# Gate and up read their token operands in runs of 512 columns, their weight blocks and first loads are begun inside the attention's output product, and less of that product lies beside attention

## The chip, the cores and the metric

The kernel runs on one core of one Trainium2 chip. The metric is the device time of one execution in microseconds (us), and lower is better. The kernel is written in a tile framework: the program names tiles in pools (SBUF, or PSUM for the eight accumulator banks), and the framework puts each instruction on its engine's queue and inserts the waits. In the profile PE is the matrix engine, PEld its weight loads, DVE the vector engine, ACT the scalar engine, POOL the GpSimd engine, SP the engine that issues most DMA. The names with a q (SPq) are the DMA queue's own sequencer.

## What is computed

The reference is one adaptive-layernorm transformer block over 2 batches of 1024 tokens, 1024 features, 32 heads of 32:

```python
mod = silu(c) @ wmod                       # 6 vectors of 1024 for each batch: shift, scale, gate, twice
h   = layernorm(x) * (1 + scale1) + shift1
q, k, v = split(clip(h @ Wqkv.T, -8, 8))   # q and k are layernormed over all 1024 features
p   = softmax(q @ k.T / sqrt(32) + alibi_bias, causal)
x1  = x + gate1 * ((p @ v) @ Wout.T)
h2  = layernorm(x1) * (1 + scale2) + shift2
act = silu(h2 @ Wg.T * ag) * (h2 @ Wu.T * au)      # 2752 inner features; Wg, Wu, Wd hold only -1, 0 and 1
out = x1 + gate2 * (act @ Wd.T * ad)
```

## The kernel before

The work runs in five stages: the modulation and the qkv product of batch 0; attention, with the other products of the two batches woven between its matmuls; the rest of the attention's output product; gate and up of batch 0 and then of batch 1; and the down product.

**Seven products.** The qkv, output, gate and up products each cut a 2 x 2 block product into seven products of half-size operands (Strassen's form). The list `SEVEN` gives their order. A token operand (`TOKEN_OPS`, seven for 256 tokens: four blocks or differences of blocks of the transposed h2, and so on) is formed once, by `token_operands`, split into a rounded high part and a remainder (`hl`, a tile of 128 partitions x 2 parts x 4 k-blocks x 128 columns, two buffers) and stored to `hop2_dram` in HBM. Gate and up read it back as seven tiles `hs_0` to `hs_6` of 2 MB for each batch. Each holds one operand of all four pairs of token tiles (NJ = 4 pairs j of 256 tokens). In the kernel before, the order inside a partition of `hs` is part, j, k-block, column, so that a matmul's moving operand (one part, one k, all j) is four runs of 128 columns with gaps between them.

**Attention and the woven work.** The generator `dense_work` yields the output product (`output`) for the four pairs of batch 0 and then the first two pairs of batch 1. `together` pulls from it according to `share`: DENSE0 and DENSE1 are how many us of such work, by the kernel's own count, are put beside each batch's attention. The rest of pairs (1,0) and (1,1) is finished when attention is over. Then `output` does pairs (1,2) and (1,3) alone. `operand(b, j)` loads the inverse softmax sums of a pair (`rb`, line 1202) and its attention outputs (`aoA`), multiplies them on DVE and POOL (line 1220), and forms the seven blocks. The sums of the last attention block reach `rb` through a store, a load, the reciprocal, a store (`rec`) and a load.

**From output to gate-up.** After `seven`, `output` normalises the pair (line 723 is the last step) and queues four transposes (`todo`), behind which come the operands of the pair and their stores (`hl`, lines 1180 to 1182).

**Gate and up.** `gate_up(b)` loops over 11 pairs p of 256 inner features (the last has 192, so 96 columns a half). `stage(p)` loads 2 MB of gate and up weights into two `wst` tiles (three buffers). `weight_operands` forms their seven operands: A11, A12 and A22 are copies on ACT (line 1559), S1 to S4 are sums on POOL (line 1561). In batch 0 `ternary` looks on DVE whether the weights are -1, 0 or 1. In batch 1 it does the same for the down weights, `wdst`, loaded for it alone. Seven steps e then issue 8 matmuls for gate and 8 for up into the banks gx, gy, ux, uy: 112 matmuls a pair and 2464 over both batches. Results are combined on DVE and ACT (`gP`, line 1603) and stored to `act_dram`. `ident_r` (line 1522) is a rounded identity for two `exact` probes of hs_0, done after step 0 of the first pair.

**Down.** The 11 down weight blocks are loaded (`wds`, line 1663 and later for the rest, two buffers) and rounded to `wd` on POOL and DVE in turn. For each of 16 token tiles the activations `a` are loaded on ACT's queue, split into `hi` (ACT, line 1678) and `lo` (DVE, line 1679), and 88 matmuls follow, whose moving operand is 512 contiguous columns of `wd`.

**Order.** Each engine works through its queue in order. While `pinned[0]` is true the matmuls keep program order; the framework sets the places of the other instructions. SP's loads and stores are one queue in order: one that must wait for a buffer holds up all behind it. A new tile in a used place waits for the last users of what lay there, with `reuse_waits="tile"` for the tile in question alone.

Of the kernel before, what the change touches and what calls it, by code (L numbers as in the profile page):

```python
# [480 lines left out]
def kernel(  # L481
# [81 lines left out]

    hop2_dram = [dram.tile([P, 7, 2, NJ, KC // 2, P], FP, tag=f"hs_{b}", name=f"hs_{b}") for b in range(B)]
    act_dram = [dram.tile([P, NJ, 2, NIC, P], FP, tag=f"act_{b}", name=f"act_{b}") for b in range(B)]
# [219 lines left out]
    def weights_b(pool, w, nm, sums, other=None, swap=False):  # L785
# [8 lines left out]
            )  # L794
            for q in order
        }
# [371 lines left out]
    def token_operands(b, j, h2, pool):  # L1168


        b11, b12, b21, b22 = (h2[:, ds(kh * KC // 2, KC // 2), m, :] for kh in range(2) for m in range(2))
        t = {q: pool.tile([P, KC // 2, P], FP, tag=f"t{q}", name=f"t{q}_{b}_{j}") for q in ("T1", "T2", "T3", "T4")}
        nc.vector.tensor_sub(t["T1"], b12, b11)
        nc.vector.tensor_sub(t["T2"], b22, t["T1"])
        nc.gpsimd.tensor_sub(t["T3"], b22, b12)
        nc.gpsimd.tensor_sub(t["T4"], b21, t["T2"])
        t.update(B11=b11, B21=b21, B22=b22)
        for i, q in enumerate(TOKEN_OPS):
            hl = pool.tile([P, 2, KC // 2, P], FR, tag="hl", name=f"hl_{b}_{j}_{q}", bufs=2)
            nc.vector.tensor_copy(hl[:, 0], t[q])  # L1180
            (nc.gpsimd if i % 2 else nc.vector).tensor_sub(hl[:, 1], t[q], hl[:, 0].bitcast(FP))
            nc.sync.dma_start(hop2_dram[b][:, i, :, j], hl.bitcast(FP))

# [52 lines left out]

    def output(b, js, pools, banks, bt, todo, keep, q0=1):

# [8 lines left out]
        for j in js:  # L1247
# [37 lines left out]
            yield from seven(lambda q, i: a[q][:, i, :], bt, banks, read, todo.places(q0, 1, ahead), 2)  # L1285
            yield from todo.run(len(todo.list), True)
            for m in range(2):
                nc.sync.dma_start(x1_dram[b * NT + qts[m]], xs[m])
# [14 lines left out]
    OUT_US = 112.0  # L1303
    LEAD, DENSE0, DENSE1 = 16.0, 345.0, 161.0

# [123 lines left out]
    ]  # L1429
    pinned[0] = True  # L1430
    ost = ctx.enter_context(ExitStack())
    right = {}
# [6 lines left out]
    def dense_work():  # L1439
        yield from dense0  # L1440
        yield from projections(1, qpools, banks, 1)
        early.close()
        hbp = right["hb"] = ost.enter_context(tc.tile_pool(name="hb", bufs=1))
        wop = ost.enter_context(tc.tile_pool(name="wo", bufs=1))
        gap_, tkp, partp, osm, aop = [
            ost.enter_context(tc.tile_pool(name=n, bufs=k))
            for n, k in (("oga", 1), ("tok", 4), ("opart", 1), ("osmall", 1), ("ao", 1))
        ]
        opools = (gap_, aop, tkp, partp, hbp, osm)
        operands(0, 0, opools[1])  # L1450
        bt = weights_b(wop, wout_t, "o", wt_dram[3])
        out_args.extend((opools, banks, bt, Todo(banks), keep))
        yield from output(0, range(NJ), *out_args)
        yield from output(1, range(NJ // 2), *out_args)
# [14 lines left out]
    opools, _, bt, todo, _ = out_args  # L1469
    with tc.tile_pool(name="wide", bufs=1, side="right") as wide:  # L1470
        operands(1, NJ // 2, opools[1], wide)
        in_range()
        alone(output(1, range(NJ // 2, NJ), *out_args, 3))
        alone(todo.run(len(todo.list), True))
    ost.close()
    late_pools.close()
# [32 lines left out]

    with ExitStack() as ff:  # L1510
        turns = [0]
        ffp = ff.enter_context(tc.tile_pool(name="ff", bufs=1, space=PSUM))
        BANKS = 8

        def ffbank(nm):
            turns[0] += 1
            i = (turns[0] - 1) % BANKS
            return ffp.tile([P, 512], FP, tag=f"ff{i}", name=nm)

        fcp = ff.enter_context(tc.tile_pool(name="fconst", bufs=1))  # L1520
        ident_r = fcp.tile([P, P], FR, name="ident_r")
        nc.vector.tensor_copy(ident_r, ident)

        with ExitStack() as gu:
            hsp = gu.enter_context(tc.tile_pool(name="hs", bufs=1, side="right", reuse_waits="tile"))
            wsp, stp, ptp, grp, urp, jkp = (
                gu.enter_context(tc.tile_pool(name=n, bufs=k, reuse_waits="tile"))
                for n, k in (("wops", 10), ("wst", 3), ("fpart", 1), ("gres", 2), ("ures", 3), ("junk", 1))
            )
            W_ORDER = ("A11", "A12", "S2", "S1", "S3", "S4", "A22")  # L1530

            def tokens_in(b, i, eng=nc.sync):
                t = hsp.tile([P, 2, NJ, KC // 2, P], FR, tag=f"hs{i}", name=f"hs_{b}_{i}")
                eng.dma_start(t.bitcast(FP), hop2_dram[b][:, i])
                return t

            def stage(p, eng=nc.sync):
                r0, n = PAIRS[p]
                st = []
                for kh in range(2):  # L1540
                    t = stp.tile([P, 2, KC // 2, 2 * P], FP, tag="wst", name=f"wst_{p}_{kh}")
                    for i, w_t in enumerate((wg_t, wu_t)):
                        eng.dma_start(
                            t[:, i, :, 0 : 2 * n],
                            w_t[ds(kh * D // 2, D // 2), ds(r0, 2 * n)].rearrange("(k p) f -> p k f", p=P),
                        )
                    st.append(t)
                return st

            def weight_operands(p, st, b):  # L1550
# [4 lines left out]
                }  # L1555
                W = {q: wsp.tile([P, 2, KC // 2, P], FR, tag="w", name=f"w{q}_{b}_{p}") for q in W_ORDER}
                f = {q: v.rearrange("p a k f -> p (a k) f")[:, :, 0:n] for q, v in W.items()}
# [14 lines left out]
            def gate_up(b):  # L1572
                tiles = [None] * 7
                st = [stage(0)]
                for i in range(7):
                    tiles[i] = tokens_in(b, i)
                for p in range(NPR):
                    n = PAIRS[p][1]
                    if p + 1 < NPR:
                        st.append(stage(p + 1))  # L1580
# [6 lines left out]
                    bank = {(mat, c_): ffbank(f"{mat}{c_}_{b}_{p}") for mat in "gu" for c_ in "xy"}  # L1587
                    part = {}
                    for e, (c_, qa, qb_, q) in enumerate(SEVEN):
                        done = {}  # L1590
                        for i, mat in enumerate("gu"):
                            ps = bank[mat, c_]
                            for k in range(KC // 2):
                                for hl in range(2):
                                    matmul(
                                        ps[0:n].rearrange("p (j t) -> p j t", j=NJ), W[qa][:, i, k, 0:n],
                                        tiles[e][:, hl, :, k, :],
                                        start=(q in ("P1", "P2", "P5") and k == 0 and hl == 0),
# [13 lines left out]
                        if q in QUAD:  # L1612
# [16 lines left out]
                            )  # L1629
                        if b == 0 and p == 0 and e == 0:  # L1630
                            exact(tiles[0][:, 0, 0].rearrange("p k t -> p (k t)"), NCOUNT, ffbank("probe0"), jkp)
                            exact(tiles[0][:, 1, 0].rearrange("p k t -> p (k t)"), NCOUNT + 1, ffbank("probe1"), jkp)
                            turns[0] += 2

            for b in range(B):
                gate_up(b)

        with ExitStack() as dn:
            wdp, wdst, aip, hip, lop, xp1, yp, dlp = (
                dn.enter_context(tc.tile_pool(name=n, bufs=k, reuse_waits="tile"))  # L1640
                for n, k in (
                    ("wd", 1), ("wdst", 2), ("ain", 2), ("ahi", 2), ("alo", 2), ("x1in", 2), ("yout", 2), ("dlate", 1),
                )
            )
            gb = []
            for b in range(B):
                gb.append(dlp.tile([P, D], FP, name=f"gb{b}"))
                nc.scalar.dma_start(gb[b], gate_dram[5][b].partition_broadcast(P))
            wd = []
            for p, (r0, n) in enumerate(PAIRS):  # L1650
                t = wdst.tile([P, 2, D], FP, tag="wdst", name=f"wds_{p}")
                nc.sync.dma_start(t[0:n], wd_t[ds(r0, 2 * n), :].rearrange("(m p) e -> p m e", p=n))
                w = wdp.tile([P, 2, D], FR, tag=f"wd{p}", name=f"wd_{p}")
                (nc.vector if p % 2 else nc.gpsimd).tensor_copy(w[0:n], t[0:n])
# [3 lines left out]
            def more_wd():  # L1658
                for p, (r0, n) in enumerate(PAIRS):
# [3 lines left out]
                    nc.sync.dma_start(t[0:n], wd_t[ds(r0, 2 * n), :].rearrange("(m p) e -> p m e", p=n))  # L1663
                    w = wdp.tile([P, 2, D], FR, tag=f"wd{p}", name=f"wd_{p}")
                    (nc.vector if p % 2 else nc.gpsimd).tensor_copy(w[0:n], t[0:n])
# [39 lines left out]


    work.close()
    wrong = nc.values_load(bad_i[0:1, 0:1], min_val=0, max_val=1)
# [48 lines left out]
```

## Time and profile before

| | |
|---|---|
| Time, median of 3 runs | 2469.14 us (2466.67 to 2471.86) |
| The profiled execution's own time | 2464.6 us |
| Its span in the trace | 2462.9 us (1.7 us lie outside it) |
| Mean granted clock of PE over the span | 0.956 |
| PE | 2230.4 us busy, 91% of the span, 9715 matmuls |
| DVE | 1316.0 us, 53% |
| POOL | 936.4 us, 38% |
| ACT | 812.5 us, 33% |
| DMA | 441.56 MB in 249820 packets, 179 GB/s mean |

The profile's page gives busy time, a picture of the span in 40 slices of 61.6 us (each digit the busy share in tenths), the chain of work that ended last, and groups of instructions. Around it the trace can be asked for a timeline (start, duration, engine, line, operation, output and inputs, count; in brackets the idle time ahead of it and what ended it) and for windows (for each stretch the busy time of every engine, the granted clock, the DMA share and GB/s). Consecutive matmuls of one kind are one row of a timeline. The matmuls' ends are modelled, so the time of one in a steady stream is read from the starts of rows. Landmarks of the profiled execution: attention's last matmul ends at 1350.7 us, the first gate matmul starts at 1491.2, the second batch's gate-up starts near 1790 to 1800, gate-up ends at 2091.4, the first down matmul starts at 2107.2.

### The profile page before, as it was taken

The numbers are of one execution on the slowest core, as the hardware profiler recorded it, in microseconds if no ns is written. First come the engines' busy times: TensorE is split into PE (matmuls) and PEld (weight loads), VectorE is DVE, ScalarE is ACT, GpSimd is POOL, SyncE is SP. The second block draws the span as 40 slices with busy tenths as digits, with TensorE's granted clock in tenths as the row PEclk, the third lists the DMA queues.
The fourth block names the chain that finished last, engine by engine and source line by source line (L and its number), as shares of the span: only waits on it lengthen the run. The fifth ranks groups of instructions, "written<-read, shape, count | busy, mean of one in ns | idle before, by whom it ended". The sixth has DMA issues, their size and how long they took to land.

```text
span 2462.9 us, 27003 instructions
## 1 busy us (share of the span) xinstructions
PE 2230.4 (91%) x9715; PEld 1220.5 (50%) x9715; DVE 1316.0 (53%) x1909; ACT 812.5 (33%) x1667; POOL 936.4 (38%) x709
## 2 busy tenths in 40 slices
PE   6999999999999987988897657999999999499998
PEld 2444443333333322322222225788777887388887
DVE  5775642555656432676776575777535644222221
ACT  1322224444444454545454002333323332011110
POOL 2330213332545544756665554433434431211111
PEclk9999999999999998999899877999999999799999
DMA  9886867355266217454541559434486452833331
GB/s 365 308 317 249 301 236 248 101 186 191 82 204 202 82 57 262 149 160 134 162 148 63 157 213 341 125 116 124 163 303 196 147 164 75 303 121 125 127 126 36
DMA packets 249820, 441.56 MB, mean 179 GB/s; under 512 B 12769, under 2 KB 170049, under 8 KB 238669
## 3 DMA queue, kind: packets, MB, share of 16 engines
q1 hardware_dynamic: 242840, 407.71, 48.4%
q10 hardware_dynamic: 6836, 32.03, 3.6%
q8 instruction: 79, 1.29, 0.2%
q14 instruction: 65, 0.52, 0.1%
HBM read 305.46 MB, written 134.23 MB: 179 GB/s over the span
## 4 chain that ended last, share of the span: by engine, by line
PE 38%; DMA 5%; DVE 5%; issue 5%; POOL 5%; ACT 1%; SPq 0%; POOLq 0%; DVEq 0%; ACTq 0%
PE dn L739 11%; PE gx L739 6%; PE ux L739 6%; PE uy L739 4%; PE gy L739 4%; PE bank L739 4%; DMA wds<-in_L_ffn_Wd_dram 2%; PE sc L739 1%; DMA wst<-in_L_ffn_Wu_dram 1%; DVE p L1097 1%; PE av L739 1%; DMA hs<-hl_T 1%; POOL xr L1283 1%; ACT p L1065 1%; DVE h2t L845 1%
## 5 line engine op out<-in xcount | busy, mean ns | idle before, releaser
L1065 ACT ACTIVATE p<-sc,kw 128x128 f32<-128x128 f32 (+3 forms) x1024 | 422.7, 514 | 425.3 <-PE sc L739 395.2
L739 PE MATMUL bank<-wT,a 128*128 128x512 f32 x768 | 365.4, 609 | 13.9 <-ACT P L957 8.2
L1097 POOL TENSOR_TENSOR p<-p,p 128x1024 f32<-128x1024 f32 (+3 forms) x128 | 267.5, 2090 | 214.1 <-PE av L739 187.8
L1097 DVE TENSOR_TENSOR p<-p,p 128x1024 f32<-128x1024 f32 (+3 forms) x192 | 240.5, 1266 | 127.8 <-POOL p L1069 68.3
L739 PE MATMUL bank<-wB,a 128*128 128x512 f32 x576 | 270.5, 606 | 1.5 <-DVE raw L964 0.7
L739 PE MATMUL dn<-wd,hi 128*128 128x512 f32 (+1 forms) x704 | 221.8, 397 | 28.3 <-ACT hi L1678 15.8
L739 PEld LDWEIGHTS bank<-wT,a 128*128 128x128 f32 x768 | 136.4, 191 | 198.3 <-issue 167.6
L739 PE MATMUL dn<-wd,lo 128*128 128x512 f32 (+1 forms) x704 | 220.0, 394 | 5.6 <-DVE lo L1679 5.6
L739 PE MATMUL sc<-cq,ck 32*128 32x512 f32 (+3 forms) x1536 | 189.0, 553 | 39.5 <-ACT p L1065 31.1
L1069 POOL TENSOR_SCALAR_AFFINE_SELECT p<-p 128x256 f32<-128x256 f32 x256 | 129.7, 518 | 193.8 <-ACT p L1065 183.3
L739 PE MATMUL av<-p,cv 128*32 128x512 f32 (+3 forms) x1536 | 173.8, 513 | 19.1 <-POOL p L1069 19.1
L739 PEld LDWEIGHTS bank<-wB,a 128*128 128x128 f32 x576 | 102.0, 189 | 145.8 <-issue 123.8
L1561 POOL TENSOR_TENSOR wS<-wst,wst 128x1024 fp32r<-128x1024 f32 (+1 forms) x22 | 51.9, 2359 | 311.1 <-DMA wst<-in_L_ffn_Wu_dram 198.3
L739 PEld LDWEIGHTS dn<-wd,hi 128*128 128x128 f32 (+1 forms) x704 | 133.7, 191 | 59.5 <-issue 16.2
L739 PEld LDWEIGHTS dn<-wd,lo 128*128 128x128 f32 (+1 forms) x704 | 134.1, 191 | 35.0 <-DVE lo L1679 6.3
L739 PEld LDWEIGHTS sc<-cq,ck 32*128 32x128 f32 x1536 | 64.1, 189 | 170.1 <-issue 100.5
L1696 POOL TENSOR_TENSOR y<-y,x 128x512 f32<-128x512 f32 x32 | 40.6, 1290 | 268.1 <-DVE y L1695 268.1
L1695 DVE TENSOR_TENSOR y<-dn,gb 128x512 f32<-128x512 f32 x32 | 20.6, 686 | 219.6 <-issue 196.7
L1678 ACT CAST hi<-a 128x2560 fp32r<-128x2560 f32 (+1 forms) x32 | 42.3, 1369 | 284.1 <-PE dn L739 225.3
L739 PE MATMUL gx<-hs,wA 128*128 128x512 f32 (+1 forms) x352 | 91.5, 403 | 24.0 <-ACT wA L1559 23.0
L739 PEld LDWEIGHTS av<-p,cv 128*32 128x32 f32 x1536 | 32.9, 109 | 150.1 <-issue 78.4
L739 PE MATMUL gx<-hs,wS 128*128 128x512 f32 (+1 forms) x352 | 91.4, 402 | 6.1 <-ACT gP L1603 4.8
(233 smaller groups left out, 3382.4 us busy)
## 6 DMA issues: line engine op xcount, KB each, us to landing
a<-hop SPq DMA_DIRECT2D x20, 1792.0 KB
hs<-hs SPq DMA_DIRECT2D x14, 2048.0 KB
wm<-in_L_wmod_dram SPq DMA_DIRECT2D x48, 512.0 KB
wB<-in_L_attn_Wqkv_dram SPq DMA_DIRECT2D x21, 1024.0 KB
wst<-in_L_ffn_Wg_dram SPq DMA_DIRECT2D x40, 512.0 KB
wst<-in_L_ffn_Wu_dram SPq DMA_DIRECT2D x40, 512.0 KB
a<-act ACTq DMA_DIRECT2D x16, 1280.0 KB
qk<-qs SPq DMA_DIRECT2D x16, 1024.0 KB
```

What stands on the lines that cost most here:

```text
L739: return in_order(nc.tensor.matmul(*args, **kw_))
L845: nc.vector.tensor_scalar(dst(k), tp[:, j, :], mul(k), add(k), ALU.mult, ALU.add)
L1065: last_exp[0] = nc.scalar.activation(p[:, g, lo:hi], sp[:, g, lo:hi], AF.Exp, bias=kw[:, d, h_ : h_ + 1])
L1069: last_mask[0] = nc.gpsimd.affine_select(out=p[:, :, 0:P], in_=p[:, :, 0:P], pattern=[[0, 2], [1, P]], compare_op=ALU.is_ge, fill=0.0, bas ...
L1097: adders[b](half, jb).tensor_add(dst, dst, ps[half][:, :, 0:n])
L1283: nc.gpsimd.tensor_add(xs[m][:, ts(n, HALF)], xs[m][:, ts(n, HALF)], yg)
L1561: nc.gpsimd.tensor_add(f["S1"], raw["A21"], raw["A22"])
L1678: nc.scalar.copy(hi[v[0], v[1]], a[v[0], v[1]])
L1695: nc.vector.tensor_mul(y[:, ts(n, HALF)], pss[n], gb[b][:, ts(n, HALF)])
L1696: nc.gpsimd.tensor_add(y[:, ts(n, HALF)], y[:, ts(n, HALF)], x1[:, ts(n, HALF)])
```

## The change

It has nine parts.

1. `hop2_dram` and `hs` are laid out part, k-block, j, column. A matmul of gate-up now takes `tiles[e][:, hl, k, :]`, 512 contiguous columns. The store of one `hl` puts down runs of 128 columns (512 bytes), where before each partition's part was one run of 2 KB.
2. DENSE1 goes from 161 to 133.
3. The pools of the output stage are ordered anew: `osmall`, `hb` and `tok` in `low`, the rest in `ost`. The weight blocks of `weights_b` are allocated in reverse. The pool `wide` and the separate `operands(1, NJ // 2)` ahead of the last outputs go, so that pair (1,2) is taken ahead inside pair (1,1), as the others are.
4. `stage(0)` is issued, and the pools of weights and partial results opened, ahead of the last outputs.
5. The loads of hs_0 to hs_5 are issued by `first_tokens`, called inside the last `output` after its `seven`, ahead of that pair's stores of x1 and its layernorm; hs_6 is allocated after the outputs.
6. `wst` has two buffers in place of three, and each of the seven weight operands one buffer of its own in place of ten in rotation.
7. In batch 0, matmuls are not pinned until pair 1; the two probes move from pair 0 to pair 1.
8. PSUM for gate-up is two pools of four banks, the first open during the outputs.
9. The pools of the down stage lie on the right, in the place of gate-up's, and in another order.

The core of the diff:

```diff
-    hop2_dram = [dram.tile([P, 7, 2, NJ, KC // 2, P], FP, ...) for b in range(B)]
+    hop2_dram = [dram.tile([P, 7, 2, KC // 2, NJ, P], FP, ...) for b in range(B)]
...
-            for q in order
+            for q in (reversed(order) if made else order)
...
-            nc.sync.dma_start(hop2_dram[b][:, i, :, j], hl.bitcast(FP))
+            nc.sync.dma_start(hop2_dram[b][:, i, :, :, j], hl.bitcast(FP))
...
             yield from todo.run(len(todo.list), True)
+            if after is not None and j == NJ - 1:
+                after()
...
-    LEAD, DENSE0, DENSE1 = 16.0, 345.0, 161.0
+    LEAD, DENSE0, DENSE1 = 16.0, 345.0, 133.0
...
-    with tc.tile_pool(name="wide", bufs=1, side="right") as wide:
-        operands(1, NJ // 2, opools[1], wide)
-        in_range()
-        alone(output(1, range(NJ // 2, NJ), *out_args, 3))
-        alone(todo.run(len(todo.list), True))
-    ost.close()
+    in_range()
+    ff = ctx.enter_context(ExitStack())
+    gu = ctx.enter_context(ExitStack())
+    ffp = [ff.enter_context(tc.tile_pool(name="ff_a", bufs=1, space=PSUM))]
+    stp, wsp, ptp, grp, urp = (
+        gu.enter_context(tc.tile_pool(name=n, bufs=k, side="right", reuse_waits="tile"))
+        for n, k in (("wst", 2), ("wops", 1), ("fpart", 1), ("gres", 2), ("ures", 3))
+    )
...
+    staged = [stage(0)]
...
+    def first_tokens():
+        ost.close()
+        hsp = gu.enter_context(tc.tile_pool(name="hs", bufs=1, side="right", reuse_waits="tile"))
+        token_tiles(range(6), hsp)
+
+    alone(output(1, range(NJ // 2, NJ), *out_args, 3, first_tokens))
+    alone(todo.run(len(todo.list), True))
...
-                W = {q: wsp.tile([P, 2, KC // 2, P], FR, tag="w", name=f"w{q}_{b}_{p}") for q in W_ORDER}
+                W = {q: wsp.tile([P, 2, KC // 2, P], FR, tag=f"w{q}", name=f"w{q}_{b}_{p}") for q in W_ORDER}
...
+                    if p == 1:
+                        pinned[0] = True
...
+                    if (b, p) == (0, 1):
+                        for i, mat in enumerate("gu"):
+                            exact(tiles[0][:, i, 0], NCOUNT + i, bank[mat, "y"], jkp)
...
-                                        ps[0:n].rearrange("p (j t) -> p j t", j=NJ), W[qa][:, i, k, 0:n],
-                                        tiles[e][:, hl, :, k, :],
+                                        ps[0:n], W[qa][:, i, k, 0:n], tiles[e][:, hl, k, :],
...
-            wdp, wdst, aip, hip, lop, xp1, yp, dlp = (
-                dn.enter_context(tc.tile_pool(name=n, bufs=k, reuse_waits="tile"))
+            wdst, wda, yp, xp1, gbp, _, hip, lop, wdb = (
+                dn.enter_context(tc.tile_pool(name=n, bufs=k, side="right", reuse_waits="tile"))
                 for n, k in (
-                    ("wd", 1), ("wdst", 2), ("ain", 2), ("ahi", 2), ("alo", 2), ("x1in", 2), ("yout", 2), ("dlate", 1),
+                    ("wdst", 2), ("wda", 1), ("yout", 2), ("x1in", 2), ("gb", 1), ("gap", 1),
+                    ("ahi", 2), ("alo", 2), ("wdb", 1),
                 )
             )
```

## The prediction

> **What bounds the kernel now.** I read the slices first, then the windows between attention and gate-up, then the timeline of PE at every idle stretch. The slices (PE, granted clock):
>
> ```profile
> PE   6999999999999987988897657999999999499998
> PEclk9999999999999998999899877999999999799999
> ```
>
> PE is the bound nearly everywhere (2230.4 of 2462.9 us), so matmul time counts in full, and so do the holes: slices 22 to 24 (output to gate-up) and 34 (gate-up to down). The timeline of PE names what ended each hole (start, length, instruction, in brackets the idle time before it):
>
> ```profile
> 1386.36 9.12 PE L739 MATMUL bank<-wB_o,aoA 128*128 128x512 f32 x16 [21.92 <-DVE aoA L1220]
> 1457.53 1.09 PE L742 MATMUL bank<-ident,xr 128*128 128x128 f32 x4 [9.20 <-DVE xr L723]
> 1491.18 3.78 PE L739 MATMUL gx<-hs,wA 128*128 128x512 f32 x8 [22.56 <-ACT wA L1559]
> 1500.72 1.22 PE L739 MATMUL probe<-hs,ident_r 128*128 128x512 f32 x2 [3.26 <-DVE ident_r L1522]
> 2107.21 1.19 PE L739 MATMUL dn<-wd,hi 128*128 128x512 f32 x2 [15.82 <-ACT hi L1678]
> ```
>
> Then the steady streams. Between starts of rows in gate-up, and in down:
>
> ```profile
> 1600.26 2.04 PE L739 MATMUL uy<-hs,wS 128*128 128x512 f32 x8
> 1602.14 2.03 PE L739 MATMUL gx<-hs,wA 128*128 128x512 f32 x8
> 1604.01 2.04 PE L739 MATMUL ux<-hs,wA 128*128 128x512 f32 x8
> ```
>
> ```profile
> 2200.13 0.62 PE L739 MATMUL dn<-wd,lo 128*128 128x512 f32 x2
> 2200.59 0.61 PE L739 MATMUL dn<-wd,hi 128*128 128x512 f32 x2
> 2201.04 0.62 PE L739 MATMUL dn<-wd,lo 128*128 128x512 f32 x2
> ```
>
> Gate-up: 1.874 us for 8, 234.3 ns each. Down: 0.453 for 2, 226.6 ns. Same shape, same granted clock 1.00; down's moving operand is contiguous, gate-up's is four runs.
>
> [...]
>
> **The change part by part**, against the profiled execution's 2464.6 us (4.5 below the median).
>
> *(a) Contiguous operands.* 2464 matmuls × (234.3 − 226.6) = **−19**. Bounds: 0 if the 7.7 ns come of something else (other stationary source, banks), −19 if all of it. The pair of 96 columns, with a quarter less weight to load but the same runs, still takes 230.7 to 233.4, so weight loads aren't the cause. Batch 1's first pair follows DMA, so I take −17.
>
> *(b) Fewer outputs beside attention.* Before, PE has 12.2 us of leftover output after attention (to 1364.4), then idles 21.92: the operand of (1,2) lands 35.6 us after attention ends (sums, store, reciprocal at 1360.21, store, load of `rb`). `rb` is an SP step that was late by itself:
>
> ```profile
> 1374.74 16.08 SPq L1202 DMA_DIRECT2D rb<-rec  x8
> ```
>
> After, the scheduled order leaves 14 matmuls of (1,0) and all 28 of (1,1) behind attention's last: 42 × 0.87 = 36.5 us plus transposes, about 39, so the 35.6 us are covered and the idle 21.92 goes. What remains open is how much attention shortens by giving up 28 matmuls = 24.5 us of PE. From 900 to 1352 PE is 85% busy, with waits on ACT p 29.6 and POOL p 19.1, so a part of the freed time turns into waiting. If attention gives back 15 of 24.5: 24.5 − 15 − 21.9 = **−12**. Bounds: +2.6 if nothing comes back (24.5 − 21.9 and attention as long as before), −19 if nearly all.
>
> *(c) Output to gate-up, and pair 0 to pair 1.* Before, the idles from 1457 to 1501 are 9.2 + 6.7 (between transposes) + 22.56 + 3.26. The window shows how little PE does there and how loaded DMA is (columns: PE, PEld, DVE, ACT, POOL busy, clock, DMA share, GB/s):
>
> ```profile
> 1450.00:1500.00 50.00, 10.66 (x32) 7.51 (x32) 34.61 (x56) 3.17 (x5) 22.80 (x13) 0.55 0.92 336
> ```
>
> After, weights and hs_0 to hs_5 (12 MB) are under way during and after the last output product, and PE's order puts e0 to e4 ahead of the last transposes, so the 22.56 go at first. But hs also holds the last pair's operands: as e5's and e6's tiles they need the last `hl` stores, which go out only after the layernorm. And pair 1 waits for a chain: stage(1) needs one of two `wst` buffers, freed by pair 0's ternary on DVE, which stands behind `ident_r`, which waits for the last `hl` store. Before, the last `hl` store landed about 30 us after the last transpose, because two `hl` buffers turn round at 4.4 to 6.0 us beside the hs loads:
>
> ```profile
> 1485.34 4.40 DMA hs<-hl_T
> 1493.14 5.97 DMA hs<-hl_T
> ```
>
> After it: `ident_r` 1.4, ternary 4.7, load 5, copy 1, about 12.5 us to pair 1. So pair 1 starts at the last store + 12.5, against 1526.4 before: the 22.56 reappear behind pair 0. On SP the 12 MB of hs loads now stand ahead of the last x1 stores and `hl` stores (12 MB / 380 GB/s = 32 us that they share), and the last transposes stand behind e0 to e4 on PE. Setting (b) aside, the last store lands at 1499 plus 0 to 20, so pair 1 starts at 1511.5 to 1531.5: −15 to +5, middle **−5**. Stores in 512 B runs are the unknown: if the last ones cost twice their 4.4 to 6.0 us at two in flight, seven of them add some 15, which from the middle gives +10; I put the upper bound at +12.
>
> *(d) Batch transition.* Idles at 1789 to 1868 sum to 9 us, DMA share near 1.0 (370 to 430 GB/s); hs_0's load is issued about 5 us later by SP's new order and stage(1) after hs_6: **+2**, 0 to +8. The pairs of batch 1 now pass three 2 MB-class tiles (weights twice, `wdst` once) through two buffers: load plus ternary and S1 to S4, about 24 us of turns against 26.2 us (25.4 with (a)) a pair. Covered by 1 to 2 us; if not, it is the rival R2.
>
> *(e) Down start.* Gate-up ends at 2091.4, PE is steady from 2149.1: 57.6 us for 23 us of work. SP is held by the weight loads:
>
> ```profile
> 2098.78 12.78 SPq L1663 DMA_DIRECT2D wds<-in_L_ffn_Wd_dram  x2
> 2116.13 25.85 SPq L1663 DMA_DIRECT2D wds<-in_L_ffn_Wd_dram  x7
> ```
>
> After, the first two `wds` and two x1 tiles are loaded during the last pair, so about 16 MB in place of 19 remain behind it at 345 to 380 GB/s: the last `wd` at 48 to 50 us. **−9**, bounds −16 (the first down matmul at 8 in place of 15.8 us, too) and −3.
>
> *(f) Start of the output stage.* The loads of pair (0,0), 2 MB (`rb` 1 MB, `aoA` 1 MB), were issued early and now stand on SP right ahead of the output weights, behind which attention's `ck` already waits (PE idle 8.27 at 958.3 with 332 GB/s moving). 2 MB / 332 GB/s = 6 us. PE has other waits there, so **+4**, 0 to +10.
>
> *Nothing:* W operands of pair 0 on POOL between outputs (S1, S2, S4, 7.7 us; POOL is 46% busy in that window, but it is ahead of the `xr` adds of (1,1), which end in the layernorm: up to 7.7 if that cover is gone, inside (c)'s bound); PSUM in two pools (same eight banks); the moved probes (same work).
>
> Sum: −17 − 12 − 5 + 2 − 9 + 4 = −37: 2427.6 profiled, 2432 on the median's scale; I say **2430**.
>
> **The rivals.**
> - *R1: contiguous runs bring nothing*, the rest as above: −20, some 2447. For it: [...]down differs in more than the runs. Against: same shape and clock, 7.7 ns apart throughout. Chance 0.27.
> - *R2, slower: two `wst` buffers.* In place of the stall being paid once, every pair waits for the ternary of the pair before on DVE before its load can start. Place: SP's stage(p+1) rows. Price: batch 0's load (2 MB, 6 us) + copies and sums about 9 + ternary 8 are 23 of 26 us; batch 1 adds the `wdst` turn, 24. At 2 us of miss a pair × 20 pairs = 40 the whole gain of 37 is gone (2468), which is the point from which it decides; at 3 us, 60 − 37 = +23: 2488. For it: DVE's ternary of `wdst` already held PE for 4.80 at the transition. Against: POOL waits 198 us for `wst`, so loads are mostly long there, with about 12 us of slack a pair. Chance 0.17.
> - *R3: cancelled.* The unknown ends of (c), (d) and (f) at their upper bounds with (a) at zero and the gains at their least: 0 + 2.6 + 12 + 8 − 3 + 10 = +30, 2495 at worst; with (b) and (e) at their middle, +9, 2473. It would show as stalls at three places, not in every pair. Chance 0.08.
>
> **How the numbers follow.** Main case 0.48, 2412 to 2447; R1 2432 to 2462; R3 2462 to 2495; R2 2468 to 2500. Within 0.2% (5 us, about what a measurement here can tell from no change) counts as the same. Faster: 0.48 + 0.27 + a little of the others less R1's tail = 0.75. Same 0.05, slower 0.20. The range 2408 to 2476 leaves out most of R2 and a tail below.
>
> **What would show it.** (a): 8 gate matmuls in 1.81 us between row starts; 1.87 means R1. (b): the 21.92 before `bank<-wB_o,aoA` gone, attention ending near 1335. (c): the first gate matmul ahead of the last transposes, a new idle stretch before the second pair of 10 to 25 us with DVE ternary or DMA `wst` as its releaser. (e): first `dn` within 10 us of gate-up's end. (f): over 8.27 before `sc<-cq,ck` near 958. Idle of 2 us or more before gx in every pair, released by `wst`, would be R2, and make the prediction wrong.

## The result, and the profile after

The changed kernel takes 2485.45 us (median of 6 runs, 2481.71 to 2488.08) against 2470.32 us (6 runs) for the kernel before: a ratio of 1.0061, 95% interval 1.0045 to 1.0078. It is 15 us slower, where 2430 and "faster" were forecast. Its profiled execution took 2486.3 us (span 2484.6), 21.7 us more than that of before (2464.6).

The slices of the changed kernel (PE, granted clock; 62.1 us each) show where. Counted from 0, as the prediction counts them, slices 15, 16, 18 and 20 (attention beside the output product) and 24 to 25 (the first pairs of gate-up) have lower digits than before, slices 21 to 23 (the end of attention and what follows it) and 34 (gate-up to down) higher ones.

```profile
PE   6999999999999986887878765899989999699998
PEclk9999999999999988998989988899999999799999
```

The timeline of PE in the changed kernel, the stalls that matter, in order of time (start, length, instruction, in brackets the idle time ahead and what ended it):

```profile
956.23 3.75 PE L739 MATMUL bank<-wB_o,aoA 128*128 128x512 f32 x4 [18.42 <-DMA wB_o<-in_L_attn_Wout_dram]
1364.77 8.46 PE L739 MATMUL bank<-wB_o,aoA 128*128 128x512 f32 x12 [3.13 <-DVE oU L1281]
1414.32 7.59 PE L739 MATMUL bank<-wT_o,aoS 128*128 128x512 f32 x12 [5.20 <-ACT oP L1273]
1441.66 8.83 PE L739 MATMUL bank<-wB_o,aoA 128*128 128x512 f32 x16 [4.25 <-DVE aoA L1220]
1484.61 1.09 PE L742 MATMUL bank<-ident,xr 128*128 128x128 f32 x4 [9.60 <-DVE xr L723]
1532.90 3.78 PE L739 MATMUL gx<-hs,wA 128*128 128x512 f32 x8 [7.29 <-DMA hs<-hs]
1545.48 0.77 PE L739 MATMUL gy<-hs,ident_r 128*128 128x512 f32 x1 [6.21 <-DVE ident_r L1569]
1556.70 3.78 PE L739 MATMUL gx<-hs,wA 128*128 128x512 f32 x8 [10.02 <-ACT wA L1585]
1567.97 3.75 PE L739 MATMUL gy<-hs,wA 128*128 128x512 f32 x8 [4.84 <-DVE probe L1553]
2131.63 1.19 PE L739 MATMUL dn<-wd,hi 128*128 128x512 f32 x2 [9.38 <-ACT hi L1710]
```

The idle of 21.92 us before pair (1,2) is gone, as forecast, and the first down matmul waits 9.38 in place of 15.82. New are the 18.42 us at the start of the output stage and the row of stalls between the first and the second pair of gate-up (1532 to 1568). The lengths show a second cost of these stalls: after 18.42 us of waiting four matmuls take 3.75 us, where 1.98 is usual, and the granted clock is 0.50 (from 956.30 to 959.90). After a wait of 4.14 us in gate-up, near 1894, half rate (427 ns a matmul in place of 227) lasted 4.9 us, with a granted clock of 0.50 from 1898.30 to 1903.10. After a wait of 0.87 us, from 1399.80 to 1403.00, the granted clock is 1.00. How long a wait has to be to bring half rate on was not tried.

Read as starts of the same instruction in both traces, the time goes like this (us, before and after):

| landmark | before | after | later by |
|---|---|---|---|
| first output matmul | 933.8 | 956.2 | 22.4 |
| last `av` matmul of attention | 1350.2 | 1347.5 | −2.7 |
| first matmul of output pair (1,2) | 1386.4 | 1399.8 | 13.4 |
| last output matmul | 1447.7 | 1474.4 | 26.7 |
| first gate matmul | 1491.2 | 1490.7 | −0.5 |
| second pair of gate-up | 1526.4 | 1556.7 | 30.3 |
| third pair | 1553.4 | 1591.9 | 38.5 |
| last matmul of gate-up | 2091.0 | 2121.9 | 30.9 |
| last down matmul | 2454.1 | 2475.7 | 21.6 |

### The profile page after: what moved, and what is told of

Same layout as the page of the kernel before. It is cut to its first block, busy times and chain, and to the rows that moved or that the text cites. A ratio compares the mean times of both kernels' runs of the same rounds, so it can differ in the third digit from the quotient of the medians.

```text
span 2484.6 us, 26907 instructions
## 1 busy us (share of the span) xinstructions
PE 2225.8 (90%) x9715; PEld 1222.7 (49%) x9715; DVE 1311.1 (53%) x1909; ACT 807.6 (33%) x1667; POOL 933.2 (38%) x709
## 5 line engine op out<-in xcount | busy, mean ns | idle before, releaser
L1097 DVE TENSOR_TENSOR p<-p,p 128x1024 f32<-128x1024 f32 (+3 forms) x192 | 246.6, 1297 | 147.7 <-POOL p L1069 85.3
L739 PE MATMUL bank<-wB_o,aoA 128*128 128x512 f32 x128 | 74.8, 725 | 28.6 <-DMA wB_o<-in_L_attn_Wout_dram 18.4
```

Source lines behind the costliest of these rows:

```text
L739: return in_order(nc.tensor.matmul(*args, **kw_))
L1097: adders[b](half, jb).tensor_add(dst, dst, ps[half][:, :, 0:n])
```

## The experiments

Ratios are to the kernel before on the same chip, with 95% intervals; the changed kernel's is 1.0061. Names beginning with b are the kernel before with an edit, those beginning with a the changed kernel with one. Starts quoted from profiles include a shift of up to 6 us that a run already has before the output stage (in us: changed kernel 1.0, a_161 3.9, a_ao 5.7, a_ao161 0.6, b_133 2.2).

### Gate-up's rate: the runs, the place, or the pools

**b_lay**, part 1 of the change alone:

```diff
-    hop2_dram = [dram.tile([P, 7, 2, NJ, KC // 2, P], FP, ...)]
+    hop2_dram = [dram.tile([P, 7, 2, KC // 2, NJ, P], FP, ...)]
...
-                                        tiles[e][:, hl, :, k, :],
+                                        ps[0:n], W[qa][:, i, k, 0:n], tiles[e][:, hl, k, :],
```

> The kernel before with the new token layout alone (runs of 512 columns, stores in runs of 512 bytes). Theory, the rate is all that the layout does: 8 gate matmuls in 1.81 us in place of 1.87, 19 us less (2470 to 2451), with the first pair's start within 3 us of before. Rival, the smaller store runs slow the last hl stores: the stores of hl take longer, the first pair starts 5 to 15 us later and 5 to 15 of the 19 us are lost.

Measured: 1.0022 (1.0013 to 1.0031), 5 us slower. The timeline of PE in this kernel has not moved from 1.87 us for 8:

```profile
1600.14 2.04 PE L739 MATMUL ux<-hs,wS 128*128 128x512 f32 x8
1602.01 2.03 PE L739 MATMUL gy<-hs,wS 128*128 128x512 f32 x8
1603.88 2.03 PE L739 MATMUL uy<-hs,wS 128*128 128x512 f32 x8
```

Both expectations miss: contiguous operands bring nothing at all, and the layout costs 5 us. Where those 5 us lie is only partly seen (the third pair starts 2.7 us later than the run's own shift explains). The stores are the likely place: between 1380 and 1600 us a DMA packet of 512 bytes took 27 ns here and one of 2 KB 84 ns in the kernel before (medians), so the four that now stand for one take 108. The stores alone were not tried.

**a_old**, the changed kernel with that part undone:

> The changed kernel with the operands back in four runs of 128 columns and stores of 2 KB, all else as changed (its tiles lie congruent). Theory, without the runs the rate falls back to what the shift alone gave: 26.0 to 26.1 us a pair, 12 to 15 us more, less 3 to 5 that the larger stores give back: 7 to 12 us slower than the changed kernel. Rival, the tiles' place alone makes the rate there: 25.4 us a pair, and the time within 3 us or 3 to 5 us less.

Measured: 1.0048 (1.0032 to 1.0064), some 3 us less than the changed kernel, in line with b_lay's sign, though the two intervals overlap. The timeline of PE:

```profile
1706.26 1.98 PE L739 MATMUL uy<-hs,wS 128*128 128x512 f32 x8
1708.07 1.98 PE L739 MATMUL gx<-hs,wA 128*128 128x512 f32 x8
1709.89 1.98 PE L739 MATMUL ux<-hs,wA 128*128 128x512 f32 x8
```

1.81 us for 8, with four runs of 128. The changed kernel is faster in gate-up, and the layout is not why. What is left is where its tiles lie. Worked out from the pools, the byte offsets of the stationary operand (`W`) and of the moving one (`hs`) in a partition agree modulo 512 in the changed kernel, as do `hi`/`lo` and `wd` in both down stages, also at 226.6 ns. In the kernel before `W` and `hs` differ by 352 (stationary less moving, as in all that follows). `hs` itself lies at 480 modulo 512 in both kernels; `W` lies at 320 before and at 480 after.

**b_pad**, **b_padlay**: an unused tile of 32 bytes ahead of the hs tiles, without and with the new layout (the difference becomes 384):

```diff
+            shift = gu.enter_context(tc.tile_pool(name="shift", bufs=1, side="right", reuse_waits="tile"))
+            shift.tile([P, 8], FP, name="shift")
             hsp = gu.enter_context(tc.tile_pool(name="hs", bufs=1, side="right", reuse_waits="tile"))
```

> The kernel before (operands in four runs) with one unused tile of 32 bytes a partition allocated ahead of the hs tiles, so that these lie at addresses congruent to those of the weight operands modulo 64 bytes; before, the two differ by 32 there, and in the changed kernel and in both down stages, which run at 226.6 ns, they do not. Theory, where the stationary and the moving tile lie to each other sets the 7.7 ns: 8 gate matmuls in 1.81 us, 25.4 us a pair in place of 26.24, and the time falls by 14 to 20 us. Rival, the rate comes from something else in the changed kernel (PSUM pools, one buffer for each weight operand, sides): 26.24 us a pair and no change, within 3 us.

> The kernel before with both: runs of 512 columns and the 32-byte shift, nothing else. Each alone left the pair at 26.24 (runs) or 26.1 us (shift). Theory, the rate needs both, a moving operand in one run and a stationary operand congruent to it modulo 64 bytes: 25.4 us a pair, 8 matmuls in 1.81 us, 18 us less from gate-up; 4 to 6 us of that are lost to the stores in runs of 512 bytes; in all 10 to 16 us less. Rival, the rate comes from the changed kernel's other pools: 26.0 to 26.2 us a pair, within 5 us of before.

Measured: 0.9985 (0.9977 to 0.9993) and 1.0007 (0.9998 to 1.0015). Both run pairs of 26.13 us in batch 0 and 26.03 in batch 1 (26.24 before): a small step in the right direction, the same with and without the runs. The expectation that the rate needs both was wrong. The second is 5 us slower than the first, which is the layout's cost again.

**b_pad160**: the same with `[P, 40]`, 160 bytes, so that the two agree modulo 512.

> The kernel before with one unused tile of 160 bytes a partition ahead of the hs tiles and nothing else: stationary and moving tile then agree modulo 512 bytes (before they differ by 352, with the 32-byte shift by 384). Theory, that agreement makes the rate: 226.6 ns a matmul, 25.4 us a pair in place of 26.24, 14 to 18 us less. Rival, the place has little to do with it and the changed kernel's rate comes from its short stalls or pools: 26.0 to 26.24 us a pair, less than 5 us.

Measured: 0.9935 (0.9915 to 0.9955), 16 us faster than before, by 160 bytes of unused space; `W` and `hs` now both lie at 320. The timeline of PE:

```profile
1600.12 1.98 PE L739 MATMUL uy<-hs,wS 128*128 128x512 f32 x8
1601.93 1.98 PE L739 MATMUL gx<-hs,wA 128*128 128x512 f32 x8
1603.74 1.98 PE L739 MATMUL ux<-hs,wA 128*128 128x512 f32 x8
```

**a_mis**: the reverse, 96 bytes of unused space in the changed kernel.

```diff
         ost.close()
+        shift = gu.enter_context(tc.tile_pool(name="shift", bufs=1, side="right", reuse_waits="tile"))
+        shift.tile([P, 24], FP, name="shift")
```

> The changed kernel with 96 bytes of unused space ahead of its hs tiles, so that stationary and moving tile differ by 96 modulo 512 in place of agreeing. Theory, the place makes the rate: 231 to 235 ns, 25.9 to 26.3 us a pair, 8 to 18 us slower than the changed kernel. Rival: 226.6 ns still, within 3 us.

Measured: 1.0104 (1.0082 to 1.0126), some 10.6 us slower than the changed kernel, and its timeline of PE is back at the old rate:

```profile
1720.85 2.04 PE L739 MATMUL ux<-hs,wA 128*128 128x512 f32 x8
1722.73 2.03 PE L739 MATMUL gx<-hs,wA 128*128 128x512 f32 x8
1724.60 2.04 PE L739 MATMUL ux<-hs,wA 128*128 128x512 f32 x8
```

Made in the kernel before and unmade in the changed one by the place of `hs` alone, the cause of the 7.7 ns is settled: how the two tiles lie to each other, not the runs, not the other pools, and not the place of one tile by itself, since `W` at 320 is slow beside `hs` at 480 and fast beside `hs` at 320.

### Attention and the output product

**b_133**, part 2 alone (DENSE1 from 161 to 133 in the kernel before), and **a_161**, part 2 undone:

> The kernel before with DENSE1 at 133 alone. Theory, attention gives back about 13 of the 24.5 us of PE time (as between the changed kernel at 133 and at 161), so it ends near 1337, and the 42 matmuls left over take 45 to 50 us, as in the changed kernel, because DVE and POOL, not PE, carry the output work there: pair (1,2) starts within 6 us of 1386 and the last output ends 0 to 13 us later; the time is 0 to 13 us longer. Rival, the leftover runs at PE's rate (36.5 us) and covers the inverse sums: pair (1,2) starts near 1375, 8 to 14 us less.

> The changed kernel with DENSE1 back at 161. Theory, attention is not bound by PE there, so the 28 matmuls (24.5 us) cost little beside it: attention ends within 5 us of the changed kernel's 1347.5, pair (1,2) starts 8 to 14 us earlier (near 1388, again held by the inverse sums), and the time falls by 8 to 14 us. Rival, PE bounds attention and gives the time back: attention ends 15 to 24 us later, and the time is unchanged or longer.

b_133 measured 1.0080 (1.0064 to 1.0095), 20 us slower, worse than either expectation. Attention ends at 1326.5, 23.7 us earlier: here all of the 24.5 us come back. But pair (1,2) then waits longer than ever, since its `rb` loads stand on SP behind the x1 and `hl` stores of the extra pair (timelines of PE and of SP in b_133):

```profile
1403.31 9.38 PE L739 MATMUL bank<-wB_o,aoA 128*128 128x512 f32 x16 [25.75 <-DVE aoA L1220]
```

```profile
1388.64 0.46 SPq L1288 DMA_DIRECT2D x<-xr  x1
1392.04 0.36 SPq L1182 DMA_DIRECT2D hs<-hl_T  x1
1392.45 1.38 SPq L1202 DMA_DIRECT2D rb<-rec  x2
```

a_161 measured 1.0059 (1.0038 to 1.0079): no difference from the changed kernel that its interval can tell, where 8 to 14 us less were expected. Its rival came nearer: attention ends at 1363.3, 15.8 us later, and the time is unchanged. PE waits 17.1 us at the start of the output stage, on aoS, and 31.47 us for aoA ahead of pair (1,2), where before waits 21.92. So in the changed kernel as it stands part 2 is neither the loss nor a gain by itself; with the start of the stage mended (the next two runs, against each other) it costs 6 us.

**a_ao**, the pool of attention outputs last in its stage, so that pair (0,0)'s loads have their space early as before, and **a_ao161**, the same with DENSE1 at 161:

```diff
-                (ost, "oga", 1), (ost, "opart", 1), (ost, "ao", 1), (ost, "wo", 1),
+                (ost, "oga", 1), (ost, "opart", 1), (ost, "wo", 1), (ost, "ao", 1),
```

> The changed kernel with the pool of the attention outputs placed last in its stage, as before, so that the first pair's 2 MB of loads have their space early. Theory, the 18.4 us wait for the output weights near 956 is the 2 MB ahead of them and the late start: the wait falls under 8 us, attention's matmul number 864 comes 5 to 8 us earlier and so does the end, 5 to 8 us less. Rival, attention is bound by its exponentials and makes that up by its end: within 3 us.

> The changed kernel with DENSE1 at 161 and the pool of attention outputs last in its stage. Theory, most of what was lost ahead of gate-up is these two: the wait at the start of the output stage (17.1 us on aoS with DENSE1 at 161, 18.4 on wB_o at 133) falls under 8, attention ends within 4 us of the kernel before, the last output 8 to 14 us after it in place of 26.7, and the time falls by 10 to 16 us from the changed kernel. Rival, the loss lies in what follows attention whatever the amount left over (POOL's sums for pair 0's weights, pair (1,2)'s operand taken inside (1,1)): the last output still 18 us or more behind, less than 6 us.

Measured: 1.0035 (1.0021 to 1.0050), 6 us less than the changed kernel as expected, though the wait on `wB_o` only fell to 11.2; and 1.0010 (1.0002 to 1.0017), 12.6 us less, inside its expectation, though PE still waits 9.8 us at the start of the stage where under 8 was expected. In a_ao161 attention ends at 1351.4, like before, and the last output matmul comes 11.2 us behind before in place of 26.7. What is left is again pair (1,2)'s operand (timeline of PE):

```profile
1397.31 9.16 PE L739 MATMUL bank<-wB_o,aoA 128*128 128x512 f32 x16 [31.62 <-DVE aoA L1220]
```

The reciprocal of the last sums, which that operand waits for, comes 15.9 us after attention's end, where before has 9.8. On DVE a layernorm step stands ahead of it and waits for POOL, and on POOL a sum for pair 0's weights (part 4) stands ahead of what it waits for (timelines of POOL and DVE in a_ao161):

```profile
1362.02 2.34 POOL L1589 TENSOR_TENSOR wS<-wst 128x1024 fp32r<-128x1024 f32 x1
1366.96 0.69 DVE L705 BATCH_NORM_STATS2 st_f<-xr 128x6 f32<-128x512 f32 x1 [5.43 <-POOL xr L1283]
1367.57 0.94 DVE L1118 RECIPROCAL rc<-rc 128x128 f32<-128x128 f32 x1
```

How much of it comes of part 4 and how much of part 3, which takes this operand inside (1,1), was not tried.

### From the first to the second pair of gate-up

**a_x1**, the hs loads called after the last pair's two x1 stores:

```diff
-            if after is not None and j == NJ - 1:
-                after()
             for m in range(2):
                 nc.sync.dma_start(x1_dram[b * NT + qts[m]], xs[m])
             xn = xs
+            if after is not None and j == NJ - 1:
+                after()
```

> The changed kernel with the loads of hs_0 to hs_5 called after the last pair's two x1 stores, not ahead of them. Theory, the second x1 store stands behind 12 MB of hs loads, and the last layernorm step, which writes in place over what that store reads, waits for it: then both transposes of the last pair come ahead of the first gate matmul, the last layernorm step moves from 1521 to about 1483, the second pair of gate-up starts near 1530 in place of 1556.7, and the time falls by 18 to 27 us. Rival, the stretch is bound by the 14 MB of hs loads whatever the order: less than 8 us.

Measured: 1.0059 (1.0042 to 1.0076), within 1 us of the changed kernel: the theory fell, and the rival (less than 8 us) stands. The mechanism moved as said (the last layernorm step at 1487.9 in place of 1521.4, both transposes ahead of the first gate matmul), but the second pair still starts at 1556.2. The timeline of SP shows why: the next `hl` stores now stand behind the load of hs_6, which cannot be issued for 19 us, and the last of them goes out at 1541.33 (1541.21 in the changed kernel).

```profile
1504.81 19.10 SPq L1501 DMA_DIRECT2D hs<-hs  x1
1527.08 2.04 SPq L1182 DMA_DIRECT2D hs<-hl_T  x2
...
1541.33 0.37 SPq L1182 DMA_DIRECT2D hs<-hl_T  x1
```

It is not the load of hs_6 as such: in the changed kernel an act store is held at the same place of the queue for 17.69 us (from 1504.46), and in the kernel before a weight load for 17.66 us (from 1498.18), each time within 8 us of the last of four hs loads in a row.

**a_noter**, without the ternary test of pair 0's weights, probes at pair 2:

```diff
-                if b == 0:
+                if b == 0 and p > 0:
                     for kh in range(2):
...
-                    if (b, p) == (0, 1):
+                    if (b, p) == (0, 2):
```

> The changed kernel without the ternary test of pair 0's gate and up weights (that part of the computation is left out), and with the two probes at pair 2. Theory, pair 1 is held by a chain: the last hl store, ident_r, the ternary of pair 0 that frees the two wst buffers, the load, the copy: with the test out the load of pair 1 is issued before the last hl store, pair 1 starts within 3 us of pair 0's end (near 1540 in place of 1556.7), pair 2 near 1566 in place of 1592, 17 to 26 us less. Rival, the load of pair 1 is held by the DMA queue behind the hs loads and stores in any case: pair 1 near 1550, less than 10 us.

Measured: 1.0018 (1.0011 to 1.0025), 10.6 us less than the changed kernel, between the two expectations. The second pair starts 71.9 us after the last output matmul in place of 82.3, and without a wait, as the theory said: so the chain through the ternary is worth 10.4 us, about all that the run gains. The third pair starts 97.7 us after it in place of 117.4, but that is no further gain: the probes have left the second pair, which now takes 25.9 us in place of 35.2, and the pair that has them takes 36.4, because there too they meet the DVE's ternary tests (timeline of PE):

```profile
1587.63 3.75 PE L739 MATMUL gy<-hs,wA 128*128 128x512 f32 x8 [7.94 <-DVE probe L1553]
```

### A version faster than both

**b_paddown2**, **b_best** and **b_best160** are the kernel before with the down pools laid for early loads and, ahead of the hs tiles, 32 bytes, 32 bytes with the new layout, and 160 bytes with four runs.

```diff
-            wdp, wdst, aip, hip, lop, xp1, yp, dlp = (
+            aip, yp, xp1, gap, wdst, gbp, dlp = (
                 dn.enter_context(tc.tile_pool(name=n, bufs=k, reuse_waits="tile"))
...
+            wda, hip, lop, wdb = (
+                dn.enter_context(tc.tile_pool(name=n, bufs=k, side="right", reuse_waits="tile"))
```

> The same 32-byte shift, and the pools of the down stage laid so that the first two down weight blocks and the x1 tiles lie over space that is free during the last pair. Theory: the shift gives 14 to 20 us and the earlier loads a further 5 to 9, as in the changed kernel (where the down stage lagged 9.3 us less than gate-up's end); first down matmul within 10 us of gate-up's end; 19 to 29 us less in all, faster than both kernels. Rival, the down stage stays bound by the 16 MB behind gate-up's end: less than 3 us beyond the shift.

> The kernel before with the runs of 512 columns, the 32-byte shift and the pools of the down stage laid for early loads. Theory, the three add: 10 to 16 and 8 to 12 us, 18 to 28 us less than before (some 2440 to 2450), faster than both kernels. Rival, they overlap: the pairs of gate-up, now shorter, become bound by the ternary tests on DVE and the loads, and less than 15 us come out.

> The kernel before with the 160-byte shift and the pools of the down stage laid for early loads, operands still in four runs. Theory: 14 to 18 us from the rate and 8 to 11 from the down stage, 22 to 29 us less, near 2441, faster than both kernels. Rival, without the agreement modulo 512 being the cause, as with the 32-byte shift: 10 to 12 us less.

Measured: 0.9956 (0.9942 to 0.9969), 0.9963 (0.9950 to 0.9976) and 0.9899 (0.9883 to 0.9915). The down pools add 7 to 11 us (0.9985 to 0.9956; 1.0007 to 0.9963; 0.9935 to 0.9899). The layout costs less here than elsewhere: b_best is 1.7 us behind b_paddown2, within their intervals. Both missed their expectations, because the shift of 32 bytes was the wrong one. The last is 2444.10 us against 2466.91 on its chip: 23 us faster than the kernel before and, by the ratios, some 40 faster than the changed one.

## Why the prediction was wrong, point by point

The sum forecast −37; the profiles say +21.6. By stretches of the landmark table:

| step | forecast | measured | from |
|---|---|---|---|
| (b) and (f), beside attention | −15 + 4 | −2.7 | start to the last `av` matmul |
| (b), behind attention | +24.5 − 21.9 | +29.4 | last `av` matmul to last output matmul |
| (c) | −5 | +3.6 | last output matmul to second pair |
| the moved probes | 0 | +8.2 | second pair to third pair |
| (a) and (d) | −17 + 2 | −7.6 | third pair to gate-up's end |
| (e) | −9 | −9.3 | gate-up's end to last down matmul |

**(b) failed, and with it the sign.** It took the work left over behind attention to run at PE's rate, cover the wait of 21.92 us and cost nothing to pairs (1,2) and (1,3). Of the 35 us that (b) and (f) are off together, 8 lie beside attention and 27 behind it.

- *Beside attention* the time given back was put at 15 us, less 4 for (f). The 15 was about right: between a_161 and the changed kernel it is 15.8, or 12.9 after each run's own shift. (f) was too small: after its shift a_161 is still 9 us behind the kernel before at attention's end, and a_ao161, with the pools mended, less than 1. That is the start of the stage, where PE waits 18.42 us on `wB_o` (4.2 in b_133; 8.3 on `ck` and 2.4 on `wB_o` before). The prediction also looked at how busy PE is there (84% from 900 to 1352, not 85%) and at its waits on `p`. From 898 to 1352 us (us in total, times, longest) they were before:

```profile
PE sc L739 <- ACT p L1065: 29.6, 26, 3.8
PE av L739 <- POOL p L1069: 19.1, 9, 3.7
```

and after:

```profile
PE sc L739 <- ACT p L1065: 42.1, 35, 3.8
PE av L739 <- POOL p L1069: 24.8, 13, 6.3
```

  They grew by 18 us, as a part of the freed time was expected to do. But they don't tell what comes back: b_133 has the same waits (42.1 and 24.9) and its attention ends 23.7 us earlier than before. The granted clock from 900 us to attention's end was 0.89 in the changed kernel, 0.93 in b_133 and 0.91 before; why it differs, and how much of the time it explains, stays open.
- *The leftover* was put at 39 us of PE work at full rate. From the last `av` matmul to pair (1,2) it took 52.3 us (36.2 before): 8.4 us of short waits on DVE and POOL steps, and rows begun at half rate behind them (12 matmul records in 8.46 us at 1364.77, where 5.3 is usual; granted clock 0.50 from 1366.0 to 1370.5).
- *Pairs (1,2) and (1,3)* were costed at nothing. They took 74.6 us in place of 61.4; PE's waits there, on `oP`, `aoA` and h2t above all, add to 17.6 us in place of 4.9. Where PE had stood still ahead of them for 22 to 32 us they took 61.4 to 62.5 (before, b_133, a_161, a_ao161), where it had not, 74.5 (a_ao). So part of the wait that (b) counted as gone comes back behind it. POOL's sums for pair 0's weights (2.3 us each) alone don't make this, since a_161 has them too; what share they have beside the leftover's DVE and POOL steps was not tried.

Of the 29.4 us behind attention, 19.4 are part 2 (the changed kernel against a_161). The other 10 are in a_161 too: the wait ahead of (1,2), 31.47 in place of 21.92.

**(c) came out at +3.6, inside its range of −15 to +5.** The chain was the one named: last `hl` store, `ident_r`, ternary, load, copy. Its timing is plain on DVE and SP in the changed kernel's timelines:

```profile
1545.15 0.23 DVE L1569 CAST ident_r<-ident 128x128 fp32r<-128x128 f32 x1 [3.98 <-DMA hs<-hl_T]
```

```profile
1541.21 0.36 SPq L1182 DMA_DIRECT2D hs<-hl_T  x1
1549.98 0.37 SPq L1490 DMA_DIRECT2D wst<-in_L_ffn_Wg_dram  x1
```

From `ident_r` to the second pair it is 11.6 us (forecast 12.5). The last store landed near 1545: 70.7 us after the last output matmul, 51.5 before, so 19 of the "0 to 20" that the text left open, where the middle was taken. One reason given was false: hs of batch 0 holds no operand of the last pair, which is of batch 1. The stores are late because SP issues them behind 12 to 14 MB of hs loads, and a_x1 shows that moving these behind the x1 stores does not help.

**The moved probes were put at nothing ("same work"); the second pair, where they now stand, takes 8.2 us longer than before.** In the kernel before they stood in the first pair with two PSUM banks of their own, and PE waited 3.26 us there, for `ident_r`. Now they use the banks gy and uy of the second pair, and DVE reads them out only after that pair's ternary test (timeline of DVE in the changed kernel):

```profile
1564.72 2.29 DVE L1544 TENSOR_SCALAR_CACHE_REDUCE junk<-wst 128x2048 bf16<-128x2048 f32 x1
1567.12 0.69 DVE L1553 SCALAR_TENSOR_TENSOR probe<-gy,hs 128x512 bf16<-128x512 f32 x1
```

So PE waits 4.84 us for gy (1567.97, shown above) and loses some 2 us at half rate behind it (rows of 3.75 and 2.37 us for 8 matmuls, where 1.98 is usual). Half rate behind the wait of 10.02 us at the pair's start (rows of 3.78 and 2.85 us, granted clock 0.50 from 1556.7 to 1561.0) makes up another 2.6 us.

**(a): near the right rate for the wrong reason.** Matmuls did fall to 226.7 ns (timeline of PE in the changed kernel),

```profile
1715.71 1.98 PE L739 MATMUL gx<-hs,wA 128*128 128x512 f32 x8
1717.53 1.98 PE L739 MATMUL ux<-hs,wA 128*128 128x512 f32 x8
1719.34 1.98 PE L739 MATMUL gx<-hs,wA 128*128 128x512 f32 x8
```

and R1, that contiguous runs bring nothing, is nonetheless what the runs showed (b_lay, a_old). That the new pools happened to bring the tiles to agree was luck. Comparing with the down stage found the gap; choosing the runs as its cause, with the tiles' place not considered, was the error. Only 7.6 of the 15 us came out. The rate gives about 16 from the third pair on; (d), the transition's first three pairs, took 2 back, as forecast, and short stalls on DVE's `uP2r` in batch 0 and ACT's `uU` in batch 1, up to 0.8 us each, some 5.

**(e) was right**, −9.3 for −9, and b_paddown2, b_best and b_best160 confirm 7 to 11 us for the pools.

**R2 did not happen:** no pair after the third waits for `wst`; two buffers were enough there. The place of the loss was R3's, stalls at several places, which had 0.08; but R3 had (a) at zero and (e) at its least, and its loss in (b) stopped at +2.6. Parts 6 to 8 were not undone one at a time.

## What to carry to other kernels

Before work is moved out from beside another stage, price it in both places. Here 24.5 us of PE work cost 13 to 26 us beside attention (12.9 between a_161 and the changed kernel, 13.5 between a_ao161 and a_ao, 25.9 between the kernel before and b_133, each after the runs' own shifts) and 19 to 42 us behind it (19.4, 19.2 and 41.7): behind it, its DVE and POOL steps and its stores stood in the way of the next operands.

Before a layout is changed for a matmul's rate, compare the byte offsets of stationary and moving tile in the fast and the slow stream; here an unused tile of 160 bytes was all that it took (from 234.3 to 226.7 ns). When a load is moved ahead of stores in one queue, follow the last store, not the first load: here the first gate matmul came 0.5 us earlier and the second pair 30.3 us later. And a small step that is moved (the probes) has to be asked what it will find on its engine, and whose buffers it will hold.

## What the runs showed of the hardware

In these runs the time of a 128x512 matmul of gate-up or down in a steady stream, with a weight load each, went with how the two operands' offsets differ modulo 512 bytes: 226.7 ns at 0 (changed kernel, a_old, b_pad160, both down stages), 234.3 at 352 and at 96 (before, b_lay, a_mis), 233.3 in batch 0 and 232.4 in batch 1 at 384 (b_pad, b_padlay). In the slow streams the intervals repeat, at 352 for instance as 231, 234, 235, 234, 231, 238, 237 ns; in a steady stretch of the fast one all are 226 or 227. Since 384 is slow, agreement modulo 128 is not enough. A difference of 256 was not tried, so agreement modulo 256 may do. Whether the moving operand is one run of 512 columns or four of 128 made no difference at either place. The output product, at 429 ns a matmul record in an undisturbed row, shows no such effect: its tiles differ by 288 and 160 before and by 0 after, and the 429 ns stay.

The layout with its stores of `hl` in runs of 512 bytes in place of 2 KB cost about 5 us in two pairs of kernels (b_lay and before, b_padlay and b_pad); in two others (the changed kernel and a_old, b_best and b_paddown2) it was 3 and 2 us, within the intervals.
